# Start and end of a 128-graph attention kernel: the first two graphs interleaved piece by piece, a root taken graph by graph, scores moved ahead in the last slice

## The chip, the core and the metric

The kernel runs on one core of a Trainium2 chip. The metric is the device time of one execution in microseconds (us), as the median of several runs. The engines are named as in the profile: PE is TensorE's matmul, PEld its weight load, DVE VectorE, ACT ScalarE, POOL GpSimd; SPq and ACTq are the queues of SyncE and ScalarE that issue DMAs.

## The reference, cut to what matters

There are 128 graphs of 128 nodes with 768 features, 12 heads of 64. Everything is float32.

```python
h = jnp.maximum(_layernorm(x, axis=-1), 0.0)        # eps 1e-5, no gain
q, k, v = (split_heads(h @ W + b) for W, b in ...)  # W is 768 x 768
s = q @ k.T / sqrt(64) + beta * adj
s = jnp.where(adj > 0, s, -9e15)
out = x + merge_heads(softmax(s) @ v)
```

`x` is 128 x 128 x 768, `adj` 128 x 128 x 128; attention is within a graph.

## The kernel before

**Groups and slices.** The graphs are worked on in 32 groups `G` of four (`GRP`). A group has three projection slices: `qk0` (heads 0 to 5 of q and k), `v`, and `qk1` (heads 6 to 11). A slice is a product of 4 x 128 rows by 768 by 768 columns, cut into blocks of 256. All slices but the very first are done as 15 block products (`PRODUCTS`, in `product`) on sums of blocks: the sums of activations are tiles `S..` (`sum_acts`), the sums of weights are tiles `T..` (`sum_weights`). The 15 products accumulate in four PSUM banks, one for each chain a, b, c, d. A product's first use of an output block is written by ACT (line 392), each later one is added by DVE (line 396, in v lines 382 and 387). The next product of the same chain writes the same bank, so it waits until that evacuation has been done.

**The very first slice.** `plain_slice(0, "qk0")` does 18 plain block products, since the sums don't exist yet. Its block `r = j = 0` works on graphs 0 and 1 (`r` is the pair of graphs, `j` the block of columns, `k` the block of the contraction) and is split by graph. For these two graphs the layernorm is taken by rows: `rows_1` has two `bn_stats` (line 565), `bn_aggr` (567), an addition of eps (569) on DVE, and the root on POOL (571). `rows_2` has for each of three pieces `k` one DVE operation that subtracts the mean and divides (line 579), two PE transposes (584) and one ACT relu that writes the operand `A0k` (589). Ahead of it PE runs 18 matmuls on the identity (`WARM`, line 595, 36 records in the profile, since a float32 matmul has two).

**Other graphs.** Graphs 2 and 3 of group 0 and groups 1 and 2 use another way: `stats` on 32-row blocks, `moments_1` (a small matmul for the mean), `moments_2` (a small matmul for the variance, then the root as a power on POOL, line 262, and the shift, line 264). ACT then normalizes block by block (`norm`, line 308), and DVE transposes blocks (`to_hT`, line 315). Later groups use `row_stats` and `row_moments`.

**Attention.** `scores` makes the scores of three pairs of heads into six banks (line 417), DVE caps them and adds the bias (421), and ACT takes the exponential (424). `attend` multiplies with v (452), `weigh` reads the row sums and divides (429 to 439), POOL adds x (457) and SP stores. In the last slice (`qk1` of the last group) this is done by halves of two graphs as soon as blocks are ready: `scores_half` (lines 465 to 479, with its own load of x) and `attend_half` (lines 489 to 499). The order of that slice's products is `LAST`; which half goes behind which product is a list at lines 732 to 737. Below, "(5,1)" is the half `r = 1` of the block of heads `oc = 5`.

**Order.** Tile's scheduler orders each engine's queue by the program's order and by what it takes to be ready. `tc.issue_after(ins)` adds an edge that puts the instructions traced inside it behind `ins` if they are on the same engine; it adds no wait. After the last slice, DVE tests the flags (`over`, line 742), PE sums them (744) and DVE writes `bad` (745); a branch on it (lines 57 and 58) is not taken with these data.

Of the kernel before, what the change touches and what calls it, by code (L numbers as in the profile page):

```python
# [17 lines left out]
P = 128  # L18
# [96 lines left out]
def direct(ctx, tc, x, adj, wq, bq, wk, bk, wv, bv, beta, out, bad):  # L115
# [135 lines left out]
    def moments_2(G, lo, hi, mean, d):  # L251

        n = hi - lo
        for q in range(0, P, HD):
            nc.tensor.matmul(pm[G, lo][q:q + HD, 1], mean8.rearrange("p a i -> p (a i)")[:, q:q + HD], d,
                             start=True, stop=True)
        ve = stat.tile([P, n], F32, tag="ve", name=f"ve_{G}_{lo}", bufs=2)
        nc.vector.tensor_reduce(ve, pm[G, lo][:, 1], AX.X, ALU.add)
        give(pm[G, lo, "bank"])
        nc.vector.tensor_scalar(ve, ve, -1.0, EPS, op0=ALU.mult, op1=ALU.add)  # L260
        r = stat.tile([P, n], F32, tag="rstd", name=f"rstd_{G}_{lo}", bufs=2)
        nc.gpsimd.tensor_tensor(r, ve, nhalf.to_broadcast([P, n]), ALU.pow)  # L262
        t = stat.tile([P, n], F32, tag="shift", name=f"shift_{G}_{lo}", bufs=2)
        shifted = nc.gpsimd.tensor_tensor(t, mean, r, ALU.mult)
        for b in range(lo, hi):
            rstd[G, b], shift[G, b] = r[:, b - lo:b - lo + 1], t[:, b - lo:b - lo + 1]
        return shifted
# [192 lines left out]
    def scores_half(G, oc, r):  # L460

        u, j = oc // 3, oc % 3
        g0 = G * GRP + 2 * r
        t = xo[G, oc, r] = work.tile([P, 2, P], F32, tag="xo", name=f"xo_{G}_{oc}_{r}", bufs=3)
        nc.sync.dma_start(t, x[g0:g0 + 2, :, oc * P:(oc + 1) * P].rearrange("g n d -> n g d"))
        ps = [take() for i in range(2)]
        t = qk[G, f"qk{u}", r, j]
        for g in range(2):
            for i in range(2):
                h = slice(i * HD, (i + 1) * HD)  # L470
                for k in range(0, N, HD):
                    nc.tensor.matmul(ps[i][k:k + HD, g * N:(g + 1) * N], t[h, 1, g * N + k:g * N + k + HD],  # L472
                                     t[h, 0, g * N:(g + 1) * N], start=True, stop=True)
        e = es[G, oc, r] = work.tile([P, 2, 2, N], F32, tag="e", name=f"e_{G}_{oc}_{r}", bufs=6)
        for i in range(2):
            nc.vector.scalar_tensor_tensor(e[:, i], ps[i][:, 0:2 * N].rearrange("p (g n) -> p g n", g=2), SCORE_CAP * ISCALE, biasT[G][:, 2 * r:2 * r + 2, :],  # L476
                                           op0=ALU.min, op1=ALU.add)
            give(ps[i])
            nc.scalar.activation(e[:, i], e[:, i], AF.Exp, scale=1.0 / ISCALE)

    def attend_half(G, oc, r):
# [8 lines left out]
                                     vt[G, "v", r, h // 4][:, 4 * g + h % 4, :], start=True, stop=True)  # L490
        divide = weigh(G, oc, r, pa, o)

        def store():
            divide()
            give(bank)
            t = xo[G, oc, r]
            nc.vector.tensor_add(t, t, o.rearrange("p (b j) d -> p b (j d)", j=2))  # L497
            g0 = G * GRP + 2 * r
            nc.sync.dma_start(out[g0:g0 + 2, :, oc * P:(oc + 1) * P].rearrange("g n d -> n g d"), t)

        if r == 1 and oc == 4:
            stores.append(store)
        else:
            store()

    def attention(G, u):

# [12 lines left out]
    def plain_slice(G, sl, todo):  # L520

        n = 0
        for r in range(2):
            for j in range(3):
                bank = take()
                p = bank.rearrange("p (i w) -> p i w", i=2)

                parts = (slice(0, N), slice(N, H2)) if r == j == 0 else (slice(0, H2),)
                for at, k in [(at, k) for at in parts for k in range(3)]:
                    a, b = A[G, f"A{r}{k}"], wt[sl, f"B{k}{j}"]  # L530
                    for i in range(2):
                        for c in range(2):
                            last = nc.tensor.matmul(p[:, i, at], b[:, c, i * P:(i + 1) * P], a[:, c, at],  # L533
                                                    start=(k == 0 and i == 0 and c == 0), stop=(c == 1),
                                                    skip_group_check=True)
                    if at is not parts[-1]:
                        if k == 2:
                            with tc.issue_after(last.ins):
                                second()
                        continue  # L540
                    if k == 2:
                        t = qk[G, sl, r, j] = work.tile([P, 2, H2], F32, tag="qk", name=f"{sl}_{G}_{r}_{j}", bufs=8)
                        oc = j + 3 * int(sl[2])
                        for i in range(2):
                            nc.scalar.activation(t[:, i, :], p[:, i, :], AF.Identity, bias=bqk[:, i, oc:oc + 1])
                        give(bank)
                    for f in todo.get(n, ()):
                        f()
                    n += 1


    adj_0 = load_adj(0)
# [1 line left out]
    load_weights("v", AS_SUMMED)  # L554
    first = {}

    def rows_1(g):

        t = xg[0, g].rearrange("p b f -> p (b f)")
        s = stat.tile([P, 2, nc.vector.BN_STATS_DIM], F32, tag="strow_0", name=f"strow0_{g}", bufs=2)  # L560
        for h in range(2):
            with ExitStack() as behind:
                if g:
                    behind.enter_context(tc.issue_after(first["ve"].ins))
                nc.vector.bn_stats(s[:, h, :], t[:, h * VH:(h + 1) * VH])
        mv = stat.tile([P, nc.vector.BN_AGGR_DIM], F32, tag="mvrow_0", name=f"mvrow0_{g}", bufs=2)
        nc.vector.bn_aggr(mv, s)
        ve = stat.tile([P, 1], F32, tag="verow_0", name=f"verow0_{g}", bufs=2)
        first["ve"] = nc.vector.tensor_scalar(ve, mv[:, 1:2], EPS, None, op0=ALU.add)
        r = stat.tile([P, 1], F32, tag="rsrow", name=f"rsrow_{g}", bufs=2)  # L570
        nc.gpsimd.tensor_tensor(r, ve, nhalf, ALU.pow)
        return mv, r

    def rows_2(g, mv, r):

        v = xg[0, g].rearrange("p b (j c) -> p c (b j)", c=NC)
        for k in range(3):
            n = work.tile([P, 2, P], F32, tag="e", name=f"rows_{g}_{k}", bufs=6)
            first["dve"] = nc.vector.tensor_scalar(n, v[:, 2 * k:2 * k + 2], mv[:, 0:1], r, op0=ALU.subtract,
                                                   op1=ALU.mult)  # L580
            bank = take()
            p = bank[:, 0:H2].rearrange("p (c i) -> p c i", c=2)
            for c in range(2):
                nc.tensor.transpose(p[:, c, :], n[:, c, :], ident)  # L584
            name = f"A0{k}"
            if not g:
                A[0, name] = work.tile([P, 2, H2], F32, tag=name, name=f"{name}_0", bufs=1 + (k > 0))
            t = A[0, name][:, :, g * N:(g + 1) * N]
            nc.scalar.activation(t, p, AF.Relu)
            give(bank)  # L590


    warm = take()
    for n in range(WARM):
        nc.tensor.matmul(warm[:, 0:P], ident, ident, start=True, stop=True)  # L595
    give(warm)
    got = [rows_1(g) for g in range(2)]
    rows_2(0, *got[0])

    def second():  # L600


        rows_2(1, *got[1])

        nc.gpsimd.tensor_scalar(beta_c, beta_c, ISCALE, None, op0=ALU.mult)
        fold = const.tile([P, SQ], F32, name="fold")
        nc.vector.tensor_reduce(fold, ident.rearrange("p (a i) -> p i a", i=SQ), AX.X, ALU.add)
        nc.vector.tensor_scalar(mean8, fold[:, None, :].to_broadcast([P, NB, SQ]), -0.125, None, op0=ALU.mult)
        for v in vring:
            nc.gpsimd.memset(v[:, :, HD:VE], 1.0)  # L610

    def half(step):

# [5 lines left out]
        else:  # L619
# [2 lines left out]
                norm(0, g)  # L622
            for k in range(3):
                first["dve"] = to_hT(0, 1, k)

    def behind_rows(f, *args):

# [19 lines left out]
    for G in range(NG):  # L647
# [25 lines left out]
        if not G:  # L673
            load_weights("qk1", AS_SUMMED)
            then(0, lambda: behind_rows(half, 0))
            then(3, lambda: half(1))
            then(4, lambda: half(2))
            for n in range(len(SUMS_A)):
                then(n + 5, lambda n=n: after(sum_acts, 0, n))
            for n in range(len(SUMS_B)):  # L680
# [51 lines left out]
        for at, f, *args in (  # L732
            (0, load_xo, 0), (0, load_xo, 1), (0, load_xo, 2), (0, attend, 0), (2, attend, 2), (4, attend, 1),
            (9, scores_half, 5, 0), (10, scores_half, 4, 0), (11, attend_half, 5, 0), (12, scores_half, 3, 0),
            (12, attend_half, 4, 0), (13, scores_half, 3, 1), (13, attend_half, 3, 0), (14, scores_half, 5, 1),
            (14, attend_half, 3, 1), (14, scores_half, 4, 1), (14, attend_half, 5, 1), (14, attend_half, 4, 1),
        ):
            then(at, lambda f=f, args=args: f(G, *args))
        slice_of(G, "qk1", todo, LAST)

    over = stat.tile([P, 20], F32, tag="over", name="over", bufs=1)
# [136 lines left out]
```

## Time and profile before

| what | value |
|---|---|
| median of 4 runs | 2884.82 us (2884.73 to 2885.13) |
| the profiled execution | 2884.85 us, span 2883.1 us |
| PE / PEld busy | 2872.2 us / 2014.5 us |
| DVE / ACT / POOL busy | 1957.2 / 806.9 / 315.7 us |
| DMA | 218.31 MB |
| granted PE clock | 1.0 |

The span is what the profiler recorded between the first and the last instruction; 1.75 us of the profiled execution's time lie outside it. Times in the timeline are counted from the span's start. "Idle before" is an engine's idle time ahead of a group, with what released it. PE's record of a matmul overlaps that of the next, so the distance between starts counts, not the duration of one.

### The profile page before, as it was taken

What the parts mean: (1) busy time and instruction counts of PE and PEld (TensorE: products, weight loads), DVE (VectorE), ACT (ScalarE), POOL (GpSimd) and SP (SyncE); (2) the same over time, 40 slices, a digit from 0 to 9 for tenths busy, and PEclk for the clock granted to TensorE, in tenths of its full rate; (3) what the DMA queues carried; (4) which work ended last, traced back from release to release, by engine and by line L of the source; (5) the groups of instructions that cost most, each with busy time, mean ns of one, the idle gap of its engine ahead of it and who ended that gap; (6) DMA issues with size and microseconds to landing.
All of it is one profiled execution on the core that took longest, in us unless ns stands there. A gap on an engine that the chain in (4) does not pass through costs nothing.

```text
span 2883.1 us, 81559 instructions
## 1 busy us (share of the span) xinstructions
PE 2872.2 (100%) x35330; PEld 2014.5 (70%) x35330; DVE 1957.2 (68%) x4511; ACT 806.9 (28%) x1750; POOL 315.7 (11%) x304
## 2 busy tenths in 40 slices
PE   9999999999999999999999999999999999999999
PEld 7666677666677676776667766777666676666776
DVE  7866666666666666666766667666666666666665
ACT  2432322222222323313232132322223222322221
POOL 1111011111011010110101101011101111110110
PEclk9999999999999999999999999999999999999999
DMA  6222233222232222322223323233222232222311
GB/s 167 77 61 77 58 85 87 73 71 67 75 88 79 65 74 68 87 86 64 76 65 86 90 60 81 60 85 88 69 75 62 80 88 75 70 70 72 88 41 39
DMA packets 413467, 218.31 MB, mean 76 GB/s; under 512 B 110384, under 2 KB 412720, under 8 KB 413104
## 3 DMA queue, kind: packets, MB, share of 16 engines
q1 hardware_dynamic: 411232, 212.66, 26.8%
q8 instruction: 277, 4.54, 0.7%
q10 hardware_dynamic: 1872, 0.40, 0.1%
q14 instruction: 86, 0.70, 0.1%
HBM read 162.14 MB, written 50.33 MB: 74 GB/s over the span
## 4 chain that ended last, share of the span: by engine, by line
PE 99%; DVE 0%; ACT 0%; POOL 0%; issue 0%; ACTq 0%; POOLq 0%; DVEq 0%
PE bank L371 85%; PE bank L452 6%; PE bank L417 6%; PE bank L533 1%; PE bank L595 0%; ACT x L308 0%; POOL rstd L262 0%; PE bank L472 0%; DVE qk L396 0%; DVE qk_T L206 0%; DVE S L321 0%; PE bank L489 0%; DVE e L476 0%; PE bank L584 0%; DVE xo L497 0%
## 5 line engine op out<-in xcount | busy, mean ns | idle before, releaser
L371 PE MATMUL bank<-S,qk_T 128*64 128x256 f32 x7056 | 822.4, 379 | 0.8 <-ACT qk L392 0.8
L396 DVE TENSOR_TENSOR qk<-qk,bank 128x512 f32<-128x512 f32 x630 | 426.7, 677 | 410.6 <-PE bank L371 405.2
L371 PEld LDWEIGHTS bank<-S,qk_T 128*64 128x64 f32 x7056 | 503.9, 137 | 256.0 <-ACT e L424 5.2
L392 ACT ACTIVATE qk<-bank,bqk 128x256 f32<-128x256 f32 x756 | 315.8, 469 | 1149.1 <-PE bank L371 962.8
L457 POOL TENSOR_TENSOR xo<-xo,o 128x512 f32<-128x512 f32 x189 | 252.3, 1335 | 2077.2 <-DVE o L436 1749.1
L371 PE MATMUL bank<-A,qk_T 128*64 128x256 f32 x4032 | 478.6, 379 | 0.9 <-DVE qk L396 0.9
L371 PE MATMUL bank<-S,qk_B 128*64 128x256 f32 x4032 | 478.2, 379 | 1.0 <-DVE qk L396 1.0
L371 PE MATMUL bank<-v_T,S 128*64 128x256 f32 x3584 | 421.8, 380 | 0.0
L424 ACT ACTIVATE e<-e 128x512 f32<-128x512 f32 x378 | 227.8, 628 | 642.8 <-DVE e L421 641.8
L371 PEld LDWEIGHTS bank<-A,qk_T 128*64 128x64 f32 x4032 | 284.3, 137 | 137.4 <-DVE qk L396 1.1
L387 DVE TENSOR_TENSOR v<-v,bank 128x512 f32<-128x512 f32 x320 | 219.8, 687 | 232.5 <-PE bank L371 230.8
L371 PEld LDWEIGHTS bank<-S,qk_B 128*64 128x64 f32 x4032 | 278.6, 137 | 128.9 <-DVE qk L396 1.5
L371 PEld LDWEIGHTS bank<-v_T,S 128*64 128x64 f32 x3584 | 254.7, 137 | 130.4 <-issue 5.7
L421 DVE SCALAR_TENSOR_TENSOR e<-bank,biasT 128x512 f32<-128x512 f32 x378 | 231.8, 682 | 109.1 <-PE bank L417 109.1
L371 PE MATMUL bank<-v_B,S 128*64 128x256 f32 x2048 | 243.2, 379 | 0.0
L371 PE MATMUL bank<-v_T,A 128*64 128x256 f32 x2048 | 237.9, 379 | 0.0
L308 ACT ACTIVATE x<-x,block 128x192 f32<-128x192 f32 x464 | 217.9, 535 | 41.7 <-DMA block<-row 41.4
L452 PEld LDWEIGHTS bank<-v,e 128*64 128x64 f32 x6048 | 208.6, 138 | 27.3
L315 DVE STREAM_TRANSPOSE A<-x 128x256 f32<-128x256 f32 x378 | 211.8, 612 | 4.0 <-ACT x L308 4.0
L452 PE MATMUL bank<-v,e 128*64 128x65 f32 x6048 | 208.3, 221 | 0.0
L382 DVE TENSOR_TENSOR v<-bv_b,bank 128x512 f32<-128x512 f32 x192 | 131.8, 686 | 104.4 <-PE bank L371 104.3
L371 PEld LDWEIGHTS bank<-v_B,S 128*64 128x64 f32 x2048 | 147.1, 137 | 73.9
(90 smaller groups left out, 1604.4 us busy)
## 6 DMA issues: line engine op xcount, KB each, us to landing
x<-in_x_dram SPq DMA_DIRECT2D x504, 96.0 KB, 2.6
xo<-in_x_dram SPq DMA_DIRECT2D x189, 256.0 KB, 3.0
out_dram<-xo SPq DMA_DIRECT2D x189, 256.0 KB, 2.6
half<-in_x_dram SPq DMA_DIRECT2D x232, 192.0 KB, 2.8
adj<-in_adj_dram SPq DMA_DIRECT2D x128, 64.0 KB, 3.0
block<-row SPq DMA_DIRECT2D x464, 1.0 KB, 1.7
qk_T<-in_L_gnn_Wq_dram SPq DMA_DIRECT2D x10, 128.0 KB, 3.8
qk_T<-in_L_gnn_Wk_dram SPq DMA_DIRECT2D x10, 128.0 KB, 3.7
```

Of the source, the lines that this page charges most:

```text
L308: nc.scalar.activation(t, t, AF.Relu, bias=shift[G, n], scale=rstd[G, n])
L315: last = nc.vector.transpose(t[:, :, g * N:(g + 1) * N].rearrange("p c (b i) -> p c b i", i=SQ), src)
L371: nc.tensor.matmul(p[q:q + HD, i, :], lhs[:, q:q + HD], rhs, start=(first and i == 0 and c == 0), stop=(c == 1), skip_group_check=True)
L382: added[G] = nc.vector.tensor_tensor(o4, bias[:, None, :, :].to_broadcast([P, 2, 4, HD]), p.rearrange("p g (h d) -> p g h d", d=HD), ALU.a ...
L387: added[G] = nc.vector.tensor_tensor(o, o, got, ALU.add if sign > 0 else ALU.subtract)
L392: nc.scalar.activation(t[:, i, :], p[:, i, :], AF.Identity, bias=bqk[:, i, oc:oc + 1], scale=float(sign))
L396: added[G] = nc.vector.tensor_tensor(t, t, p, ALU.add if sign > 0 else ALU.subtract)
L417: nc.tensor.matmul(ps[oc, i][k:k + HD, g * N:(g + 1) * N], t[r, 1, at][:, k:k + HD], t[r, 0, at], start=True, stop=True)
L421: taken[0] = nc.vector.scalar_tensor_tensor(e, ps[oc, i].rearrange("p (g n) -> p g n", g=GRP), SCORE_CAP * ISCALE, biasT[G], op0=ALU.min, ...
L424: nc.scalar.activation(e, e, AF.Exp, scale=1.0 / ISCALE)
L452: nc.tensor.matmul(pa[q:q + HD, 2 * g + i, :], es[G, oc, i][:, 2 * r + g, q:q + HD], vt[G, "v", r, h // 4][:, 4 * g + h % 4, :], start=Tru ...
L457: nc.gpsimd.tensor_add(t, t, o.rearrange("p a (b j) d -> p (a b) (j d)", j=2))
```

## The change

It has three places. At the start, the work for graphs 0 and 1 is put in an order written out by hand: each DVE and PE instruction is chained to the one before (`line`), DVE goes on with the first graph's pieces between the second graph's statistics, and on PE two pieces are transposed ahead of a graph's first block product and the third ahead of its second. The two small matmuls of `half(1)` and `half(2)` are put behind the product before them. In `moments_2` the power and the shift are taken for four columns (one graph) at a time, in group 0's second pair of graphs and in groups 1 and 2. In the last slice the scores of (5,1) go ahead of the last product, the divisions of (3,1) and (4,1) are split off (`finish`), and division and addition of (3,1) are put behind the last scores on DVE; the addition and the store of (5,1) and all of (4,1) go behind `over`.

```diff
@@ moments_2
-        nc.gpsimd.tensor_tensor(r, ve, nhalf.to_broadcast([P, n]), ALU.pow)
         t = stat.tile([P, n], F32, tag="shift", name=f"shift_{G}_{lo}", bufs=2)
-        shifted = nc.gpsimd.tensor_tensor(t, mean, r, ALU.mult)
+        for at in range(0, n, NB):
+            one = slice(at, at + NB)
+            nc.gpsimd.tensor_tensor(r[:, one], ve[:, one], nhalf.to_broadcast([P, NB]), ALU.pow)
+            shifted = nc.gpsimd.tensor_tensor(t[:, one], mean[:, one], r[:, one], ALU.mult)
@@ scores_half
-            nc.vector.scalar_tensor_tensor(e[:, i], ...
+            taken[0] = nc.vector.scalar_tensor_tensor(e[:, i], ...
@@ attend_half
-        def store():
+        def finish():
             divide()
             give(bank)
+
+        def store():
             t = xo[G, oc, r]
             nc.vector.tensor_add(t, t, o.rearrange("p (b j) d -> p b (j d)", j=2))
             ...
-        if r == 1 and oc == 4:
+        if r == 0:
+            finish()
+            store()
+        elif oc == 5:
+            finish()
             stores.append(store)
         else:
-            store()
+            stores.extend((finish, store))
@@ plain_slice
+                for g, at in enumerate(parts):
+                    for k in range(3):
+                        if len(parts) == 2:
+                            for piece in PIECES[g, k]:
+                                transposed(*piece)
+                        ...
+                                line("pe", nc.tensor.matmul, p[:, i, at], b[:, c, i * P:(i + 1) * P], a[:, c, at], ...)
@@ the first two graphs
+    def line(engine, f, *args, **kwargs):
+        with ExitStack() as behind:
+            if engine in first:
+                behind.enter_context(tc.issue_after(first[engine].ins))
+            first[engine] = f(*args, **kwargs)
+        return first[engine]
+    PIECES = {(0, 0): ((0, 0), (0, 1)), (0, 1): ((0, 2),), (0, 2): (), (1, 0): ((1, 0), (1, 1)), (1, 1): ((1, 2),),
+              (1, 2): ()}
+    def transposed(g, k):
+        bank = take()
+        p = bank[:, 0:H2].rearrange("p (c i) -> p c i", c=2)
+        for c in range(2):
+            line("pe", nc.tensor.transpose, p[:, c, :], chunk[g, k][:, c, :], ident)
+        ...
+        nc.scalar.activation(A[0, name][:, :, g * N:(g + 1) * N], p, AF.Relu)
+        give(bank)
@@ begin(): the order on DVE
+        stats_of(0, 0)
+        stats_of(0, 1)
+        root(0)
+        stats_of(1, 0)
+        piece(0, 0)
+        stats_of(1, 1)
+        piece(0, 1)
+        root(1)
+        piece(0, 2)
         for k in range(3):
+            piece(1, k)
@@ main
     for n in range(WARM):
-        nc.tensor.matmul(warm[:, 0:P], ident, ident, start=True, stop=True)
+        line("pe", nc.tensor.matmul, warm[:, 0:P], ident, ident, start=True, stop=True)
...
-            then(3, lambda: half(1))
-            then(4, lambda: half(2))
+            then(3, lambda: behind_product(half, 1))
+            then(4, lambda: behind_product(half, 2))
@@ the last slice
-            (12, attend_half, 4, 0), (13, scores_half, 3, 1), (13, attend_half, 3, 0), (14, scores_half, 5, 1),
+            (12, attend_half, 4, 0), (13, scores_half, 3, 1), (13, attend_half, 3, 0), (13, scores_half, 5, 1),
             (14, attend_half, 3, 1), (14, scores_half, 4, 1), (14, attend_half, 5, 1), (14, attend_half, 4, 1),
         ):
             then(at, lambda f=f, args=args: f(G, *args))
+        for n in range(2):
+            then(14, lambda: behind_scores(stores.pop(0)))
         slice_of(G, "qk1", todo, LAST)
```

`behind_product` is `issue_after` the last PE instruction of the first slice's line, `behind_scores` is `issue_after(taken[0])`. The weights' and inputs' loads at the start, `WARM`, and all code of groups 3 to 30 stay as they are.

## The prediction
> **What bounds the kernel.** I read the page's busy times first, then PE's waits, then the timeline of the three places that the change touches.
>
> ```profile
> PE 2872.2 (100%) x35330; PEld 2014.5 (70%) x35330; DVE 1957.2 (68%) x4511; ACT 806.9 (28%) x1750; POOL 315.7 (11%) x304
> ```
>
> ```profile
> PE bank L371 <- DVE qk L396: 1.9, 2, 1.0
> PE bank L489 <- ACT e L479: 0.9, 2, 0.6
> PE bank L371 <- ACT qk L392: 0.8, 1, 0.8
> ```
>
> PE is the bound: of 2883.1 us it is busy for 2872.2. What can be won is the 10.9 us in which it isn't: 2.2 before its first matmul, 0.8 and 1.9 at three waits near 76 to 101 us, and the end, where PE's stream is over at about 2873.4 and DVE finishes alone. An edit counts only if it changes PE's stream, one of these waits, or that end.
>
> **Start: the order on DVE.** Of before's timeline, first 45 us:
>
> ```profile
> 7.81 2.81 DVE L579 TENSOR_SCALAR rows<-x,mvrow,rsrow 128x256 f32<-128x256 f32 x6
> 8.68 0.74 PEld L584 LDWEIGHTS bank<-ident,rows 128*128 128x128 f32 x6
> 9.20 0.94 ACT L589 ACTIVATE A<-bank 128x256 f32<-128x256 f32 x3 [5.44 <-PE bank L584]
> 9.64 2.75 PEld L533 LDWEIGHTS bank<-A,qk_T 128*128 128x128 f32 x24 [0.23 <-ACT A L589]
> 12.31 0.69 PEld L584 LDWEIGHTS bank<-ident,rows 128*128 128x128 f32 x6
> 13.28 2.75 PEld L533 LDWEIGHTS bank<-A,qk_T 128*128 128x128 f32 x24 [0.27 <-ACT A L589]
> ```
>
> The same in the chain that ended last:
>
> ```profile
> 2.15 6.80 PE bank L595 x36
> 8.95 0.71 PE bank L584 x6
> ```
>
> The root of graph 0 is ready at 6.96 (POOL, 6.40 + 0.56); DVE reaches its first piece only at 7.81, behind the second graph's statistics. With the change it starts near 7.0, 0.8 us earlier. But that piece is ready at 7.81 + 0.50 = 8.31 already before, and PE's first weight load of it is at 8.68, without a wait, since PE is in the 36 records of the warm-up until then. The warm-up is unchanged, so the first transpose stays where it is and the 0.8 us are worth 0. Of the other pieces the last is ready about 11.1 instead of 10.6, and PE wants graph 1's first at 12.31: covered by 1.2 us.
>
> **Start: the order on PE.** Before, PE transposes all three pieces of a graph (six records) while ACT makes the first relu; then it waits 0.23 and 0.27 us for that relu. The first product needs transpose, relu, operand; this starts at 8.68 and ends at 9.64 however many transposes stand behind. The change puts four transposes there; the other two stand behind the first product. PE waits longer for the relu and then does two more records inside its stream. Six records took 0.71 us in the chain, 0.118 each, so this costs 2 x 0.118 = 0.24 us for each graph and +0.47 for both. If the two fell into other waits it would be 0; if each of four stood exposed for the 0.277 us of its own record, 1.1. I take 0.47, since the chain counts starts, not overlapped durations. The Trainium skill ("TensorE: Matmul & The Clock Gate", Part 4) says that such a transpose costs about 275 ns in a kernel's context; as the price of a moved one it would make the term 1.1 and the time 2886.3. Here it is the length of one record.
>
> Later PE steps have no wait that could give the 0.47 back. The weights of the next block, issued at 11.27 and 11.74 with 2.8 us to landing, are there at 14.5, wanted at 15.95. The SP queue isn't reordered. `half` 1 and 2 stay behind the same products, at 17.88 and 20.03; `fold` and `mean8` are done by about 11.7, needed at 17.88.
>
> **The root graph by graph.** Powers took 1.673 us for 8 columns and 2.904 for 16, that is 0.154 a column and 1.06 for 4. In group 0 the first norm, at 22.83, comes at 20.84 + 1.06 + 0.08 + 0.20 + 0.04 = 22.2, 0.6 earlier. PE used the result at 27.16 without losing time: worth 0. For group 2 (POOL at 152.49) PE has no wait at all: 0. For group 1:
>
> ```profile
> 65.43 2.91 POOL L262 TENSOR_TENSOR rstd<-ve,nhalf 128x16 f32<-128x16 f32 x1 [42.64 <-DVE ve L260]
> 68.88 7.12 ACT L308 ACTIVATE x<-x,shift,rstd 128x192 f32<-128x192 f32 x16 [25.03 <-POOL shift L264]
> 75.91 1.53 ACT L392 ACTIVATE qk<-bank,bqk 128x256 f32<-128x256 f32 x4
> 76.77 3.67 PE L371 MATMUL bank<-S,qk_T 128*64 128x256 f32 x32 [0.77 <-ACT qk L392]
> ```
>
> From the table by windows (length, then busy time of PE, PEld, DVE, ACT, POOL):
>
> ```profile
> 94.00:98.00 4.00, 3.08 (x54) 2.28 (x50) 4.00 (x14) 1.81 (x8) 0.75 (x1) 1.00 0.30 84
> 98.00:101.00 3.00, 2.00 (x18) 1.11 (x20) 3.00 (x5) 0.00 (x0) 0.52 (x1) 1.00 0.54 135
> ```
>
> ACT's 16 norms hold back the evacuations of line 392, and PE waits 0.77 us for them. With four columns the first norm starts at 65.43 + 1.06 + 0.08 + 0.2 to 0.4 + 0.04, near 66.9, 2.0 us earlier. A later root with its shift takes at most 1.64, less than the 7.12 / 4 = 1.78 of four norms, so ACT doesn't stop; it is through at 74.0, and the evacuation is done before PE asks at 76.0. The wait of 0.77 goes. What is late next is DVE: from 74.35 to 101 it is busy without a gap, a queue that starts with the scores (line 421, released by PE at 74.35) and doesn't depend on these norms any more. PE's two waits of 0.92 and 1.0 us at 97 and 100 end when DVE's additions at 97.28 and 100.19 end. If PE comes 0.77 earlier it waits 0.77 longer there. So the term is 0; it is -0.77 if the scheduler moves those additions forward, as far as -1.9 if both waits went.
>
> DVE is also exposed to POOL in this stretch: the operation of line 203 at 89.75 took 1.76 us where its like took 0.68, begun 0.08 us after POOL's addition of 1.29. The Trainium skill ("GPSIMD Reference", Key points) says that POOL contends with DVE operations that have two SBUF inputs; by it the longer chain of powers (8 instructions for 2) would slow DVE. The rows say not: line 206 ran its usual 0.68 at 66.25, under the old power. I take 0, and 1.08 as the price of one more such collision.
>
> **The end.** Of the chain that ended last:
>
> ```profile
> 2871.69 1.75 PE bank L371 x16
> 2873.46 0.69 DVE qk L396
> 2874.15 0.67 DVE e L476 x2
> 2876.30 0.34 DVE e L476
> 2877.48 0.42 DVE xo L497
> 2878.43 0.18 DVE over L742
> 2879.01 0.43 DVE xo L497
> ```
>
> After the last product DVE is busy without a real gap from 2873.46 to 2879.44; the last store and the end follow in 3.66 us, which I leave unchanged (bad, at 2878.91, isn't last). The scores of (5,1) cost PE 0.60 and now stand ahead of the last product: it ends at 2874.04. Their two DVE operations (0.66) leave the queue behind it and fit in front, where DVE has about 0.9 idle by then. So far +0.60 - 0.66. But behind the product only (4,1)'s scores remain for DVE, and these need the addition (done 2874.75), PE's 0.67 us and a handover: 2875.52, while the three small operations of (3,1) end at 2875.25. A hole of 0.27 is new, since the division of (3,1), which filled it, must now stand behind the scores. From there, by the distances between starts: scores 2 x 0.33, row sums 0.48, division 0.33, division and addition of (3,1) 0.45 + 0.35, row sums 0.60, `over` 0.09, addition of (5,1) 0.35, division 0.45 with `bad` 0.10, addition 0.43. That ends at 2879.8, +0.38. The addition of (5,1) now stands between `over` and the last division. Bounds: -0.1 if the hole is filled, +0.7 if each operation costs its full 0.42. On SP the stores of (3,1) and (5,1) come 1 to 2 us later, with nothing queued behind that is due, and the last issue (0.38) is still the last.
>
> **Sum.** Profiled 2884.85 (span 2883.1 and 1.75 outside; 0.03 above the median) + 0.47 + 0 + 0.38 = 2885.7.
>
> **Rivals.** (1) *The wait at 76 us is really won* (25%): DVE's order shifts, 2885.7 - 0.77 = 2884.9, or 2884.4 with the end at -0.1. For it: the wait is in the profile; against: DVE's unbroken 4.00 and 3.00. (2) *Slower through POOL* (15%): earlier evacuations move POOL's addition at 89.67 or another onto a two-input operation of DVE before 101 us. Each collision costs 1.08 and counts as soon as it lies in the unbroken stretch; 2886.8. (3) *The early pieces do shorten the start* (8%): if the warm-up ended earlier than the records say, up to -0.8: 2884.9. (4) *The scores don't go ahead* (5%): the scheduler leaves (5,1) behind the product, the end stays and only the start counts: 2885.3. My forecast has 44%. The rest, 3%, is a disturbance in all groups, 0.2 us in each of 32, that no row suggests.
>
> A difference of 0.2%, 5.8 us, is about what a measurement of this kernel can tell from no change; all five cases lie inside it. Outside I leave the 3%, 1 for faster and 2 for slower. The range runs from 2884.2 (rival 1 with a good end) to 2886.8 (one collision).
>
> **What would show it.** In the changed profile: first transpose still at 8.7; waits for line 589's successor of about 0.45 twice; the 128-column products end near 16.5; norms of group 1 from 66.9 and no PE wait at 76, but longer ones at 97 to 101; the last product ending later by 0.6 against its surroundings, and the last addition 0.4 later than the shift of the start. Wrong if the first transpose comes earlier, or if the waits near 100 don't grow.

## The result, and the profile after

The changed kernel took 2887.98 us (median of 32 runs, 2886.94 to 2888.93) beside 2885.14 us of the kernel before in the same series (52 runs, 2884.20 to 2886.29): a ratio of 1.001, 95% interval 1.0005 to 1.0015. That is 2.84 us or 0.1% more: within the 0.2% that I called no change, on the slow side, and outside my range, which ended at 2886.8. The profiled execution took 2887.54 us, its span 2885.77 instead of 2883.07.

Line numbers from here on are those of the changed kernel: 310 is `norm`, 373 `product`, 394 and 398 its evacuations, 492 to 504 `attend_half`, 573 the helper `line`, 783 `over`, 786 `bad`. First the page's busy times and the waits of PE (total, how often, the longest):

```profile
PE 2871.7 (100%) x35330; PEld 2014.2 (70%) x35330; DVE 1956.9 (68%) x4511; ACT 807.2 (28%) x1750; POOL 319.0 (11%) x318
```

```profile
PE bank L373 <- ACT qk L394: 1.5, 1, 1.5
PE bank L373 <- DVE qk L398: 1.2, 2, 1.0
...
PE bank L492 <- ACT e L482: 0.6, 1, 0.6
PE bank L573 <- DVE rows L573: 0.4, 1, 0.4
PE bank L255 <- DVE dev L248: 0.3, 1, 0.3
PE bank L573 <- ACT A L590: 0.3, 1, 0.3
```

PE and DVE do no more than before (POOL's 14 further instructions take 3.3 us), and the waits in the middle sum to 2.7 us as they did (0.8 + 1.9 then, 1.5 + 1.2 now). New are 0.4 for rows at the start and 0.3 for `dev`. The 2.70 us of the span are found by putting the same events of both traces side by side (us from the span's start):

| event | before | after | added since the last event |
|---|---|---|---|
| first product of v, group 0 | 42.90 | 42.70 | -0.20 |
| first scores of group 0 taken by DVE | 74.35 | 74.79 | +0.64 |
| PE goes on after its last wait near 101 | 100.92 | 101.38 | +0.02 |
| last addition on DVE ends | 2879.44 | 2880.31 | +0.41 |
| end of the span | 2883.07 | 2885.77 | +1.83 |

**The start**, timeline of the changed kernel (start, duration, engine, line, operation, count, and in brackets the idle time before it with what ended it; before's is in the prediction):

```profile
2.15 5.76 PE L573 MATMUL bank<-ident 128*128 128x128 f32 x36 [2.15 <-POOL ident masks.py:199]
7.76 0.44 PE L573 MATMUL bank<-ident,rows 128*128 128x128 f32 x2
8.63 0.44 PE L573 MATMUL bank<-ident,rows 128*128 128x128 f32 x2 [0.44 <-DVE rows L573]
12.66 1.16 PE L573 MATMUL bank<-A,qk_T 128*128 128x128 f32 x8 [0.26 <-ACT A L590]
15.66 1.89 PE L573 MATMUL bank<-A,qk_B 128*128 128x256 f32 x8
```

The same 36 records of the warm-up took 5.76 us here and 6.80 before, so the first transpose came at 7.76 instead of 8.79. The second piece wasn't there yet (0.44), and of the one microsecond 0.4 is left at 15.66 (16.06 before). At v's first product 0.2 is left; the other 0.2 goes to the root in group 0, below.

**The second part of the first v slice.** Of the kernel before, then of the changed one:

```profile
61.24 0.25 PE L241 MATMUL bank<-st,mean 128*64 128x32 f32 x1
...
64.00 0.19 DVE L248 SCALAR_TENSOR_TENSOR dev<-st,dev 128x32 f32<-128x32 f32 x1
64.25 0.31 PE L255 MATMUL bank<-dev,mean 128*64 128x32 f32 x4
```

```profile
61.03 0.31 PE L241 MATMUL bank<-st,mean 128*64 128x32 f32 x4
...
64.01 0.19 DVE L248 SCALAR_TENSOR_TENSOR dev<-st,dev 128x32 f32<-128x32 f32 x1
64.25 0.31 PE L255 MATMUL bank<-dev,mean 128*64 128x32 f32 x4 [0.29 <-DVE dev L248]
```

Line 255 is the small matmul for group 1's variance. It begins at the same time in both, but in the changed kernel fewer products stand ahead of it, and PE waits for `dev`. Between the starts of two matmuls there are 0.21 us all through this slice; here there are 0.67 once (63.58 to 64.25) and 0.37 once (before line 241), which makes 0.62 of the 0.64.

**The root and the norms**, first of group 1:

```profile
65.44 4.33 POOL L265 TENSOR_TENSOR rstd<-ve,nhalf 128x4 f32<-128x4 f32 x4 [42.70 <-DVE ve L260]
69.74 0.74 POOL L266 TENSOR_TENSOR shift<-mean,rstd 128x4 f32<-128x4 f32 x4
70.06 7.12 ACT L310 ACTIVATE x<-x,shift,rstd 128x192 f32<-128x192 f32 x16 [26.41 <-POOL shift L266]
77.95 3.67 PE L373 MATMUL bank<-S,qk_T 128*64 128x256 f32 x32 [1.51 <-ACT qk L394]
```

The scheduler put all four powers ahead of all four shifts. The first norm comes at 70.06, where before it came at 68.88 and where I had put it at 66.9; PE's wait for ACT doubled. And yet nothing was lost here, as the windows show (length, then busy time of PE, PEld, DVE; before's are in the prediction):

```profile
94.40:98.40 4.00, 3.83 (x60) 2.76 (x56) 4.00 (x14) 1.81 (x8) 0.70 (x1) 1.00 0.28 79
98.40:101.40 3.00, 1.96 (x18) 1.08 (x18) 3.00 (x5) 0.00 (x0) 0.58 (x1) 1.00 0.50 135
```

DVE is still busy without a gap, and PE, which came later, waited less for it: 3.83 us busy instead of 3.08.

In group 0 the same order of powers and shifts did cost something. The first norm stands 6.97 us behind the block that starts at 15.66, where before it stood 6.77 behind the one at 16.06. Near 26.7 and 27.0 two matmuls of PE then start 0.31 and 0.32 us apart instead of 0.21, and from that block to v's first product it is 27.04 us instead of 26.84. All four kernels of this case with this order on POOL show 27.04 to 27.09 there, the ten others 26.84 to 26.87. So the root costs 0.20 us in group 0.

**The end**, from the chain that ended last (start, length, what), and the one line of the timeline that belongs to it:

```profile
2872.74 1.88 PE bank L373 x16
2874.62 0.81 PE bank L492 x26
2875.43 0.66 PE bank L474 x16
2876.09 0.02 issue
2876.11 0.76 DVE e L478 x2
...
2878.13 0.43 DVE xo L502
...
2878.97 0.42 DVE xo L502
2879.39 0.03 DVE bad L786
...
2879.45 0.41 DVE o L438
...
2879.89 0.43 DVE xo L502
```

```profile
2876.11 0.76 DVE L478 SCALAR_TENSOR_TENSOR e<-bank,biasT 128x256 f32<-128x256 f32 x2 [0.27 <-PE bank L474]
```

The hole of 0.27 us is there, the addition of (5,1) stands between `over` and the last division, and the last addition is 0.41 us later than the rest. Then comes what I had left unchanged. Transfers at the end, in 40 parts of the window, with the queues' share (packets, MB, share of the engines' time); first the kernel before (window 2880.85 to 2882.9), then the changed one (2881.2 to 2883.7). The last line of each is from the window in which the last store is issued; it ends with the time from the issue to the landing:

```profile
GB/s 230 330 0 0 160 0 0 0 0 0 0 0 0 0 0 0 0 160 0 0 0 0 0 0 0 0 0 0 0 0 0 0 0 0 0 0 0 0 0 0
...
q8 instruction: 1, 0.02, 3.0%
q1 hardware_dynamic: 15, 0.00, 0.9%
...
out_dram<-xo SPq DMA_DIRECT2D x1, 128.0 KB, 1.9
```

```profile
GB/s 205 459 254 262 254 254 279 172 82 8 16 16 156 16 25 25 8 0 131 0 0 0 0 0 0 0 8 8 8 8 8 8 8 8 16 8 25 16 0 0
...
q1 hardware_dynamic: 272, 0.13, 18.2%
q8 instruction: 1, 0.02, 4.0%
...
out_dram<-xo SPq DMA_DIRECT2D x1, 128.0 KB, 3.7
```

The last store is 256 packets of 512 B on q1. Before, all but one of them have begun when the first instruction fetch starts (q8 fetches 16 KB, q14 8 KB at a time; these fetches belong to the branch, since they move with `bad` in the experiments below). After, nearly the whole store stands in the same window as the fetches. Most of it moves at about 260 GB/s, then comes a pause, and then 16 packets one at a time, 8 GB/s being one packet per part. Landing takes 3.7 us instead of 1.9, and SP's own waits at the branch (line 58; before, then after) grew by the same 1.8:

```profile
SPq L58 <- SPq L58: 0.8, 2, 0.5
```

```profile
SPq L58 <- SPq L58: 2.6, 2, 2.1
```

### The profile page after: what moved, and what is told of

It reads as the page before. It is cut to its first block, busy times and chain, and to the rows that moved or that the text cites. A ratio compares the mean times of both kernels' runs of the same rounds, so it can differ in the third digit from the quotient of the medians.

```text
span 2885.8 us, 81573 instructions
## 1 busy us (share of the span) xinstructions
PE 2871.7 (100%) x35330; PEld 2014.2 (70%) x35330; DVE 1956.9 (68%) x4511; ACT 807.2 (28%) x1750; POOL 319.0 (11%) x318
## 4 chain that ended last, share of the span: by engine, by line
PE 98%; DVE 1%; DMA 0%; issue 0%; ACTq 0%; ACT 0%
PE bank L373 85%; PE bank L419 6%; PE bank L454 6%; PE bank L573 1%; DVE A L317 0%; DMA x<-in_x_dram 0%; DVE qk_T L206 0%; DVE S L323 0%; DVE e L423 0%; PE bank L474 0%; DVE qk L398 0%; PE bank L492 0%; DVE qk_T L203 0%; DVE xo L502 0%; DVE o L438 0%
## 5 line engine op out<-in xcount | busy, mean ns | idle before, releaser
L373 PEld LDWEIGHTS bank<-v_T,A 128*64 128x64 f32 x2048 | 147.4, 137 | 73.6
```

The lines of the kernel that those rows point to most:

```text
L373: nc.tensor.matmul(p[q:q + HD, i, :], lhs[:, q:q + HD], rhs, start=(first and i == 0 and c == 0), stop=(c == 1), skip_group_check=True)
```

## The experiments

Twelve kernels in three series, each beside the kernel before: 2884.94, 2885.06 and 2885.08 us (33 runs each). Medians are of 11 runs. The intervals of the ratios are about 0.0009 to either side, 2.6 us, so I lean on the traces, and on runs whose ranges don't overlap with those of the kernel before (2884.05 to 2885.73 over the three series).

**The changed kernel with the end as before, and the kernel before with the changed end alone.** The edits are the hunks of `scores_half`, `attend_half` and the last slice's list.

> The changed kernel with the end as before (order of the last slice, divisions and stores); start and root stay changed. Theory: of the 2.7 us that the changed profile's span is longer, about 2.3 come from the end: 0.4 from a longer DVE queue behind the last product and 1.8 from the last store, which took 3.7 us to landing instead of 1.9 because its packets met the instruction fetches of the final branch. Then this kernel is about 0.5 us slower than before (0.0 to 1.0), its last store lands in 1.9 us, and its last DVE operation starts within 0.2 us of 5.6 us after the last product's end, as before. Rival (the steady part and the start carry the loss): it stays 2 us or more slower than before.

Measured 2885.71 (2885.18 to 2886.30), ratio 1.0003 (0.9994 to 1.0012).

> The kernel before with only the changed end. Theory: 2.3 us slower than before (1.5 to 2.8): 0.4 from the DVE queue and about 1.8 from a last store that lands in 3.5 us or more. Rival (start and root carry the loss): 0.4 us slower or less, and the last store lands in 1.9 us.

Measured 2887.14 (2886.84 to 2887.69), ratio 1.0008 (0.9999 to 1.0017). So about 2.2 of the 2.8 us come from the end, and no run of it overlaps with the kernel before. With the end undone the last store lands in 2.0 us, and 0.77 stay for start and root. With the end alone the stretch from PE's start near 101 to the last addition grew by 0.43, as in the changed kernel (0.41); the store was issued at 2879.36, even before that of the kernel before (2879.47), and yet its last packet came at 2882.77 instead of 2880.94.

**When does the store meet the fetches?** The next three kernels move `bad` or the last addition and nothing else. The changed kernel with `bad` behind the last addition:

```diff
-    nc.vector.tensor_reduce(bad, pf[0:1, 0:20], AX.X, ALU.max)
     with tc.issue_after(found.ins):
         for f in stores:
             f()
+    with tc.issue_after(added["last"].ins):
+        nc.vector.tensor_reduce(bad, pf[0:1, 0:20], AX.X, ALU.max)
```

> The whole change, but the write of the flag that the branch reads stands behind the last addition on DVE, so that the branch and its instruction fetches come about 0.9 us later against the last store, whose distance to the stores before it stays as close as in the changed kernel. Theory (fetches delay the store): the last store lands in about 1.9 us again and the kernel is 1 to 1.8 us faster than the changed one, so 0.9 to 1.7 slower than before. Rival (the last store is slow since three stores stand within 1.8 us): it lands in 3.5 us or more, and the kernel is as slow as the changed one or slower.

Measured 2886.06 (2885.06 to 2886.70), ratio 1.0004 (0.9995 to 1.0013): 1.1 above the kernel before, where the changed kernel was 2.8 above. The store lands in 1.8 us, although `bad` and with it the branch come later than in the changed kernel (2880.15 and 2879.35), and although the last three stores are issued within 2.0 us, as in the changed kernel (2.1). So it isn't the closeness of the stores. The kernel before with one idle operation ahead of the last addition, and with three:

```diff
             t = xo[G, oc, r]
+            if r == 1 and oc == 4:
+                for _ in range(1):     # 3 in the second kernel
+                    nc.vector.tensor_scalar(o, o, 1.0, None, op0=ALU.mult)
             nc.vector.tensor_add(t, t, o.rearrange(...))
```

> The kernel before with one more DVE operation (a multiplication by 1 of 128 x 256) between the last division and the last addition, so that the last store is issued 0.35 to 0.45 us later while the flag and the branch stay where they are. Theory (fetches delay the store): the last store lands in 3 us or more, and the kernel is 1.5 to 2.5 us slower than before, several times the delay put in. Rival (the distance between stores decides; here it grows): the store lands in 1.9 us and the kernel is 0.35 to 0.45 us slower.

> The kernel before with three short DVE operations (0.27 us each) ahead of the last addition, where one was added in the run with the store 0.3 us late: the store is 0.8 us late, `bad` unchanged. Theory of the collision (the packets queue behind the fetches and are done 2.35 us after the fetches begin, whenever they join them): nearly as long as with one operation, +2.0 to +2.6, 2887.0 to 2887.7, landing 3.0 to 3.6. Rival, that each delay counts several times over or that landing grows in proportion to it: +5, 2890. Rival, that the delay counts once and the landing of 3.7 was an accident: +0.8, 2885.9.

One operation of 0.27 us made it 2886.99 (2886.58 to 2887.53), ratio 1.0007 (0.9998 to 1.0016), 2.05 more, and the store lands in 3.8 us. Three of them made it 2886.76 (2886.05 to 2887.52), ratio 1.0006 (0.9997 to 1.0015), 1.68 more and 0.24 below my band; the store lands in 3.0. So it is a step: not a delay that counts once, nor one that grows. The records of the end, in us; the last two columns are the end of the 16 KB fetch and of the store's last packet:

```
                         bad     store   first   packets begun     16 KB fetch  last
                         begun   issued  fetch   behind it of 256  ended        packet
before                 2878.91  2879.47  2880.90        1          2881.91      2880.94
after                  2879.35  2880.34  2881.25      250          2882.89      2883.58
end undone             2879.38  2879.94  2881.34        5          2882.69      2881.41
end alone              2878.38  2879.36  2880.34      228          2882.08      2882.77
after, bad last        2880.15  2880.26  2882.02        0          2883.39      2881.72
before, store +1 op    2879.34  2880.20  2881.21      211          2882.86      2883.56
before, store +3 ops   2878.72  2880.23  2880.56      256          2882.00      2882.68
```

Two rules for this kernel's end can be read from it. The first fetch begins 1.84 to 1.99 us after `bad` does, and an undisturbed store's last packet ends 1.46 to 1.47 after its issue; so a store that is issued up to some 0.4 us behind the start of `bad` has its packets through before the fetches. The kernel before has 0.56 and sits on the edge: in the seven traces with the old end unaltered, one to five packets are late and the store lands in 1.8 to 2.3 us. The changed end has 0.98 and 0.99. Between 0.56 and the 0.85 of the run with one operation nothing was tried. And where they meet, the last packet ends 0.68 to 0.70 us after the 16 KB fetch, in all four cases. So the end of the fetch, and no longer the store's issue, sets the end, and three operations cost no more than one. Of the transfers of that kernel with three (2880.5 to 2882.9):

```profile
GB/s 0 137 0 0 0 0 0 273 0 0 94 196 307 273 273 282 282 205 248 26 0 0 0 0 9 9 9 9 9 9 145 9 9 17 17 26 0 0 0 0
...
q1 hardware_dynamic: 272, 0.13, 19.2%
```

The single packets begin in the 25th part, near 2882.0, where the 16 KB fetch ends. The Trainium skill ("DMA: Bandwidth & Descriptors", Queues, rings and completion order) says that each DMA engine serves the rings that have work in turn and changes only at the end of a packet. Shared evenly by 16 engines, a store of 256 packets gives 16 to each, and exactly 16 begin at the end of the 16 KB fetch or behind it in each of the four traces. That they are those of the engine which carries the fetch fits the row; the records don't name the engine, so this last step is inferred.

**The kernel before with `bad` last.** If the kernel before sits on the edge, is there something to win?

> The kernel before with only the reduction of `bad` put behind the last addition. Theory: in the kernel before, the store's packets end just as the fetches start, so holding the fetches back by 0.5 us frees nothing, and the end hangs on the store's landing and not on the branch: the time stays, 2885.0 to 2885.3, landing 1.9, span less last packet 2.1 to 2.2. Rival, that the branch itself sets the end: 2885.5 to 2885.7 (later by the 0.5 that `bad` is later).

Measured 2884.90 (2884.53 to 2885.19), ratio 1.0 (0.9991 to 1.0009). The branch is 0.3 us later and the time is not; the end hangs on the store's landing. The 0.18 less can't be told from none.

**The root alone, and the root in order.** The second adds an edge that puts each graph's shift ahead of the next power:

```diff
+            with ExitStack() as behind:
+                if at:
+                    behind.enter_context(tc.issue_after(shifted.ins))
+                nc.gpsimd.tensor_tensor(r[:, one], ve[:, one], nhalf..., ALU.pow)
+            shifted = nc.gpsimd.tensor_tensor(t[:, one], mean[:, one], r[:, one], ALU.mult)
```

> The kernel before with only the root taken four columns at a time. On record I had the first norm of group 1 at 66.9 us, PE's wait of 0.77 near 76 gone, and the gain given back at the two waits near 100. The changed profile shows all four powers ahead of all four shifts on POOL. Theory now: the same here, so norms start near 70.0 (1.2 later than before), PE's wait near 76 is about 1.5, and since DVE sets the pace to 101 us the time changes by less than 0.3 us. Rival: the wait is paid in full, 0.7 us slower.

> The kernel before with the root taken four columns at a time and an order edge that puts each power behind the shift before it, so that POOL does power, shift, power, shift. Theory (the step on record): the first norm of group 1 starts near 67, PE doesn't wait for ACT near 76, its waits for DVE near 97 and 100 grow from 1.9 to about 2.7 in sum, and the time stays within 0.3 us of before. Rival: 0.5 to 0.8 us faster, the wait being really won.

Alone: 2885.98 (2884.97 to 2887.02), ratio 1.0004 (0.9994 to 1.0013), norms from 70.21, PE's wait for ACT 1.9 us. In order: 2885.06 (2884.73 to 2885.50), ratio 1.0001 (0.9992 to 1.0010). The trace of the second:

```profile
67.07 7.19 ACT L313 ACTIVATE x<-x,shift,rstd 128x192 f32<-128x192 f32 x16 [23.18 <-POOL shift L269]
```

```profile
PE bank L376 <- DVE qk L401: 2.3, 2, 1.3
PE bank L376 <- ACT qk L397: 0.3, 1, 0.3
```

Now the norms start where I had put them, and PE's wait of 0.8 near 76 is gone. The 0.3 that stands there now is another wait, at 90.4; the waits for DVE near 98 and 101 grow from 1.9 to 2.3 (I had expected 2.7), and the time stays. From v's first product to PE's start behind the wait near 101 it is 58.03 us, before 58.02, and 58.04 with the root alone, where PE's wait for ACT is 1.9. So the traces show the give-back both ways. The median of the root alone is 0.92 us above the kernel before all the same. Of this 0.24 is seen in group 0 (27.09 us from the block near 16 to v's first product); the rest stays open, since the profiled execution, 2885.23, is one of the short ones and has only 0.3 us more span than before.

**The start alone, and with all three pieces ahead of the first product:**

```diff
-    PIECES = {(0, 0): ((0, 0), (0, 1)), (0, 1): ((0, 2),), ...
+    PIECES = {(0, 0): ((0, 0), (0, 1), (0, 2)), (0, 1): (), ...
```

> The kernel before with only the changed start (order of pieces on DVE and PE, and the small matmuls put behind products). The records show that the warm-up's length differs between executions: it ended at 8.67 us with before's profile and at 7.64 with the changed one's, and DVE's first work came between 4.8 and 5.3. Theory: with a warm-up that ends near 8.7, 0.47 later at the v slice's first product than before, so near 43.4; with one that ends near 7.7, where the first piece is what PE waits for, 0 to 0.5 earlier than a kernel before with such a warm-up. In the time between -0.3 and +0.5 us. Rival (the small matmuls' places in the v slice cost as in the changed profile, where the scores come 32.1 us behind the v slice's first product instead of 31.45): +0.6 us more than the start alone gives.

> As the start alone, but all three pieces of a graph are transposed ahead of its first product, as before; the order on DVE stays changed. Theory: where the warm-up ends late, 0.47 us less than the start alone costs (two records of 0.118 for each graph are back under the wait for the relu); where it ends early, PE waits for the third piece and the first product starts later than with two pieces first. Medians within 0.5 us of the start alone. Rival: no difference at all, if the transposes' place doesn't count.

Alone: 2885.67 (2885.07 to 2886.57), ratio 1.0003 (0.9994 to 1.0012). The last matmul of its warm-up happened to start at 8.98 (8.67 before, 7.64 in the changed kernel), so the pieces were all there, and the price of the order on PE shows undisturbed: 7.71 us from the first transpose to the next block, 7.27 before, +0.44. It also has the two gaps of the v slice (32.10 us from the first v product to the first scores, 31.45 before), as the rival had it, so these come from the start's edit and not from the root's. With three pieces: 2885.18 (2883.92 to 2885.69), ratio 1.0000 (0.9991 to 1.0009); the stretch of the v slice is 31.46. Over all 14 traces it is 32.09 or 32.10 in the four kernels with two pieces ahead, and 31.45 or 31.46 in the others. Line 241's four matmuls stand singly between products again, and line 255 doesn't wait:

```profile
64.43 0.31 PE L255 MATMUL bank<-dev,mean 128*64 128x32 f32 x4
```

So a different place of two pieces' transposes near 8 to 16 us moved the four small matmuls at 61 us. Presumably the scheduler's estimate of what will be ready tipped over; that wasn't tried.

**All mended, and start with root but the old end:**

> The changed kernel with its three causes mended together: three pieces of a graph transposed ahead of its first product (the moments' small matmul then isn't drawn one product forward), each shift ahead of the next graph's power on POOL, and `bad` reduced behind the last addition, so that the branch's instruction fetch starts behind the last store's packets. Theory: stretch from v's first product to the first e 31.5 us (32.1 in the changed kernel), norms of group 1 from 67.0, store's landing 1.9 us; what stays is the end's later addition, about 0.4, less up to 0.4 from the start: 2884.9 to 2885.6 beside a before of 2885.1. Rival, that the loss lies in the order of the end's DVE work or in the longer queue of the start: 2886.5 or more.

> The two mended parts without the end: start with three pieces ahead, root graph by graph with each shift ahead of the next power, end as in the kernel before. Theory: norms of group 1 from 67.0 but the first e no earlier than 74.3, since DVE's queue gives the wait back; first v product up to 0.4 earlier where the warm-up ends early: 2884.6 to 2885.2. Rival, that an earlier norm is a gain once the start is mended: PE's waits between the v slice and the first e at 101 fall by 0.7, 2884.2 to 2884.5.

With three pieces first, the ordered root and `bad` last, the changed kernel took 2885.06 (2884.26 to 2885.58), ratio 1.0 (0.9991 to 1.0009). With the three mends together the whole loss is gone, though not all of it was mended: from PE's start near 101 to the last addition it is still 0.27 us longer than before, and the stretches ahead of it are 0.29 shorter. With the old end it took 2884.95 (2884.04 to 2885.55), ratio 0.9999 (0.9990 to 1.0008). Neither beats the kernel before by anything that can be told. The first scores are 0.3 us earlier in both traces (74.05 and 74.08), and PE's waits for DVE near 100 are at 2.3 and 2.2. That 0.3 need not be a gain: the run with three pieces alone, which has the same start, has its first scores at 74.54, 0.2 later than before.

## Why the prediction was wrong, point by point

**The last store.** The step that failed is "the last store and the end follow in 3.66 us, which I leave unchanged (bad, at 2878.91, isn't last)". I saw that `bad` isn't last, but not that the distance from it to the last store, which the change stretches from 0.56 to 0.99, is what keeps the store's packets clear of the fetches. The 3.63 us after the last addition became 5.46 in the profiled executions: +1.83, two thirds of the loss and nearly all that I missed (my sum was 0.85, the span grew by 2.70). Nothing in the trace of before showed the price, but it did show 1.9 us to landing and fetches that began 0.04 us before the last packet ended; the term should have had an upper end. None of my rivals had this mechanism.

**The start, 0.47.** The order on PE was rightly sized: 0.44 where the pieces are ready, 0.11 for each of the four moved transposes. (The 275 ns of the Trainium skill, which its page gives for bf16, are near the 0.27 to 0.33 us of one record here, but not the price of a moved one.) Two things around it weren't right. "The warm-up is unchanged, so the first transpose stays where it is" failed: in the 14 profiles of this case the last matmul of the warm-up starts between 7.64 and 8.98, with the same 36 records. The cover of 0.37 us, from the first piece's 8.31 to the 8.68 of its weight load, was that of one execution, and rival 3, which I gave 8%, is partly true wherever the warm-up ends early. The run with one idle operation ahead of the last addition shows it, for it has the old start and a last matmul at 7.68:

```profile
9.06 1.29 PE L587 MATMUL bank<-ident,rows 128*128 128x128 f32 x6 [1.10 <-DVE rows L582]
```

There PE waits 1.10 us for the first piece. In the 14 traces this piece is ready 3.3 to 3.7 us behind DVE's first statistics in the old order, and 2.7 to 3.2 in the new one. And "Later PE steps have no wait that could give the 0.47 back" looked only for gains: the other place of line 241's matmuls in PE's queue, and with it the wait at line 255, added 0.62. The sum up to the first scores, +0.44, came out near my 0.47 by accident, as -0.40 at the start, +0.20 from the root in group 0, and +0.64.

**The root, 0.** The step that put the first norm of group 1, with four columns, "near 66.9" failed: I took the order of the program's text for that of POOL's queue. Had the edge been there it would have held (67.07). "0.6 earlier" for group 0's first norm and its "worth 0" failed for the same reason: against PE's stream the norm came 0.20 later and cost 0.20; with the edge the stretch is 26.84, as before. The conclusion for group 1, that DVE's unbroken work until 101 gives back whatever PE wins or loses at 76, held in both directions in the traces; the median of the root alone, 0.92 above, isn't explained by them.

**The end on DVE, 0.38.** Right: 0.41 and 0.43 in two traces, with the hole of 0.27 at its place.

**The rivals.** With the norms at 67.07 the wait at 76 went, and no time was won by it. No collision on POOL was added: line 203 took 1.76 us, as before. The scores did go ahead. (The lower end of my range, 2884.2, lay 0.2 below the 2884.4 of its own case; nothing hung on that.)

## What to carry over

A last store and the instruction fetches of a branch behind the kernel get in each other's way: here 0.27 us of delay in the store cost 2.05. Keep the write that releases the branch behind the last store's issue, or at least not far ahead of it, and when an edit moves either, look at the packets of both. A small saving of one engine ahead of a stretch in which another is busy without a gap was worth nothing here; look for that stretch first. Where an edit relies on the order within one engine's queue, put in the edge that holds it. And a cover of a few tenths near the start should be read from several executions, or be held to be as uncertain as the warm-up's length, here 1.3 us.

## What the runs showed of the hardware that I had not expected

The matmuls of the warm-up start 0.213 us apart at first (the first two 0.37) and 0.112 later, and the change comes between 5.3 and 8.1 us in the 14 traces, 3.1 to 5.9 after the first one. The granted clock in the windows' rows says 1.00 in both halves, so only the distances show it. The Trainium skill ("TensorE: Matmul & The Clock Gate", Part 1) says that PE runs at half its clock until a free-running window of about 3.4 us was busy, so that the number of cold matmuls differs from run to run. The halves agree, and so does it that the place differs, though 3.1 is a little under one window. The size of the spread doesn't agree: the same part puts it at +-500 ns, and here it is 2.8 us wide.

A two-input operation on DVE and POOL's addition get in each other's way, and which one pays differs between executions: in 12 of the 14 traces DVE, in two POOL. Of the kernel before, and of the kernel before with the changed end, whose code is the same in this place:

```profile
89.67 1.29 POOL L457 TENSOR_TENSOR xo<-xo,o 128x512 f32<-128x512 f32 x1 [20.82 <-ACT o L439]
89.75 1.76 DVE L203 SCALAR_TENSOR_TENSOR qk_T<-qk_T,qk_B 128x512 f32<-128x512 f32 x1
```

```profile
89.74 2.49 POOL L457 TENSOR_TENSOR xo<-xo,o 128x512 f32<-128x512 f32 x1 [20.90 <-ACT o L439]
89.81 0.69 DVE L203 SCALAR_TENSOR_TENSOR qk_T<-qk_T,qk_B 128x512 f32<-128x512 f32 x1
```

DVE begins 0.08 us behind POOL in the first and 0.07 in the second. In the second it isn't slowed, POOL takes 2.49 us, and DVE's next operation of this line takes 1.17 us, where in the first it takes 0.68. PE's wait near 97 is then 0.41 instead of 0.92: half a microsecond by chance, as much as the smaller terms of this whole case. What decides which one pays isn't known.
